# VectorE in written order in the first layer of a two-layer convolution kernel, with earlier loads, a moved gate mix and borders in the background

## The chip, the cores and the metric

The kernel runs on one core of a Trainium2 chip. Its time is the device time of one execution in microseconds. The kernel before took 14336.46 us (median of 3 runs, 14333.49 to 14348.35).

## What is computed

The input x is a batch of 32 images of 8 channels and 256 x 256 pixels in fp32. Layer 0 normalises x in four groups of two channels each (GroupNorm) and makes three things of the result: the outcome of 15 steps of a coupled logistic lattice (each step multiplies g by 1 - g, mixes in a 3 x 3 convolution of each channel with itself and 0.15 of the start image), a small network (3 x 3 convolution to 128 hidden channels, relu, 1 x 1 to 8 channels, sigmoid), and a gate g that chooses between the two.

```python
for _ in range(STEPS):                       # 15
    mapped = R * grid * (1.0 - grid)
    local = _conv(mapped, K_local, groups=C_OUT)
    physics = (1.0 - EPS) * mapped + EPS * local
    grid = (1.0 - BETA) * physics + BETA * drive
cml_out = jnp.clip(grid, 0.0001, 1.0 - 0.0001)
nca_out = jax.nn.sigmoid(_conv(jax.nn.relu(_conv(x, Wp, bp)), Wu, bu))
gin = jnp.concatenate([x, cml_out, nca_out], axis=1)
g = jax.nn.sigmoid(_conv(jax.nn.relu(_conv(gin, Wg1, bg1)), Wg2, bg2))
return g * cml_out + (1.0 - g) * nca_out
```

The result is added to x. Layer 1 normalises again, quantises to integers of at most 127, convolves 3 x 3 to 8 channels and adds once more.

## The kernel before, in words

Layer 0 is one stage and layer 1 the next; each has its own pools of on-chip memory. Images that pass from step to step lie in DRAM scratch tensors: `xp_s` (normalised, split in a high and a low part), `xq_s` (normalised, for the lattice), `cm_s` (lattice result), `nc_s` (network result), `y_s` (layer 0's result). Their border rows are zeroed at the start from a zero tile `zt` by 272 DMAs on ACT's queue (lines 199 and 202). `zt` lies in the preparation pool. The pools of layer 0 are opened later on the same memory, and with the plain pool setting every one of their tiles waits for all users of the preparation pool.

The 32 images are handled in 8 groups of 4. For each group four pieces of work are written as generators:

- `lattice(g)`: for each of 8 channels ("units") 15 steps; a step has three tiles, and for each tile TensorE makes six matmuls (L487) into two PSUM buffers `pt`, VectorE adds the start image (`gt`, L495) and makes the next map (`m_a` or `m_b`, L500), GpSimd clears two columns (L504). After the second and third tile, two DMAs each (`exchange`, L450 and L451) copy neighbouring rows of `m_a` for the next step. `background(3)` issues up to three waiting loads or stores of the lattice after every tile. The next unit's images are loaded from step 7 on.
- `nca(b)`: the network, by pairs of `hidden` matmuls (L567, PSUM buffers `ph` from the same pool of six), relu on ACT (L577), the small second product (L584) and a sigmoid.
- `gate(b)`: ten pairs of strips `p`. `stage` loads the network result `nb`, the lattice result `cq` and the image `xb`, GpSimd rearranges `cq` into `cmb` (L681), VectorE scales `xb` into `xnb` (L700). TensorE makes 18 matmuls from `xnb`, `cmb` and `nb` (L759); relu follows (L771). `finish` of the pair before makes the gate `pg` (L725), sigmoid (L727), on GpSimd `d` = lattice - network (L730) and `f` = x + network (L732), and on VectorE the mix gate * d + f (L734, L735) with its statistics (L743 to L745).
- `normalise(jobs)`: a job is one half (two channel pairs) of one image: load `xr`, statistics (L305), average over partitions with two small matmuls (L313, L324), a power on GpSimd (L327), scaling (L331), a rearranged copy `xq` on ACT (L336), the cast `hi` (L342), the remainder `lo` on GpSimd (L343), and six store DMAs. `hi`, `lo` and `xq` have one buffer each, `xr` four.

`together` mixes the lattice of group g with a filler: the network of group g, the gate of group g - 1 and the normalising of group g + 1. A generator's `yield w` ends a piece that counts w; pieces are drawn so that both sides advance in proportion to planned totals (`T_NCA` 520, `T_GATE` 340, `T_PREP` 34, `T_LATTICE` about 709). Before the first lattice, `prep(0, (0,))` normalises the first half of the channels of four images; their second half comes first in group 0's filler. After the last lattice the last four gates run alone.

TensorE's instructions keep the order in which the program writes them:

```python
one.enter_context(tc.manual_schedule(engines={mybir.EngineType.PE}))
```

All other engines, SP's DMA queue included, are ordered by the framework's scheduler, which may move an instruction ahead of others when it expects its inputs to be ready.

## Time and profile before

| what | value |
|---|---|
| median of 3 runs | 14336.46 us |
| profiled execution | 14416.5 us, span 14414.7 us |
| mean granted TensorE clock | 0.963 |
| TensorE busy | 13267.4 us (92%) |
| VectorE busy | 8213.1 us (57%) |
| ACT busy | 4039.8 us (28%) |
| GpSimd busy | 2445.9 us (17%) |
| L487 lattice matmuls | 5827.0 us from m_a, 5796.6 us from m_b |
| L567 hidden matmuls | 2800.2 and 2675.2 us |
| DMA share of the span, mean | 41.9% on SP's queue, 1.7% on ACT's |

The profile shows one execution. Times in it are microseconds from the span's start. A row of a timeline gives the start, the duration, the engine (SPq is SP's queue as it issues DMAs), the line, the operation, what it writes and reads, how many were merged, and in brackets how long the engine had been idle and what ended that. A row of waits gives who waited for whom, the sum, the number of times and the longest. A row of a window gives each engine's busy time and number of records, then the mean granted TensorE clock and the share and rate of the DMA engines. TensorE's records count each fp32 matmul twice. Lines are those of the kernel before.

### The profile page before, as it was taken

The page shows a single profiled execution, that of the slowest core. Times are in us where ns is not written, and L with a number is a line of the kernel's source. Part 1 is how long each engine was busy: PE and PEld are TensorE (multiplying, and loading weights), DVE is VectorE, ACT ScalarE, POOL GpSimd, SP SyncE. Part 2 cuts the span into 40 slices and gives each one's busy share as a digit, 9 for nine tenths or more (in the row PEclk, how much of TensorE's full clock was granted, in tenths as well). Part 3 has the DMA queues.
Part 4 walks back from the last instruction along what each step waited for, and adds up shares of the span by engine and source line. Part 5 has one row for each costly group of instructions (what it writes and reads, how often), then busy time and mean ns, then how long its engine had stood idle before and what let it go on. Part 6 is the DMA issues. An engine that isn't in the chain of part 4 may idle for free.

```text
span 14414.7 us, 229163 instructions
## 1 busy us (share of the span) xinstructions
PE 13267.4 (92%) x81728; PEld 6423.3 (45%) x81728; DVE 8213.1 (57%) x16290; ACT 4039.8 (28%) x6274; POOL 2445.9 (17%) x4266
## 2 busy tenths in 40 slices
PE   2999999999999999999999999999999999999833
PEld 1554444444444444444444444444444444444311
DVE  3555555555555555555555555555555555555576
ACT  1333232232222222222322223222323222222122
POOL 1111111111111111111111111111111111112300
PEclk9999999999999999999999999999999999999966
DMA  5444444444444444444444434444444433333465
GB/s 148 93 97 92 90 103 106 103 94 100 110 94 100 99 106 94 103 100 95 100 103 107 98 93 106 110 94 94 104 104 98 103 88 88 80 83 78 122 195 176
DMA packets 2259559, 1496.74 MB, mean 104 GB/s; under 512 B 1061248, under 2 KB 2229504, under 8 KB 2258304
## 3 DMA queue, kind: packets, MB, share of 16 engines
q1 hardware_dynamic: 2176976, 1401.95, 41.9%
q10 hardware_dynamic: 81456, 80.12, 1.7%
q8 instruction: 664, 10.88, 0.3%
q14 instruction: 463, 3.79, 0.1%
HBM read 866.48 MB, written 478.69 MB: 93 GB/s over the span
## 4 chain that ended last, share of the span: by engine, by line
PE 70%; DMA 9%; DVE 9%; SPq 5%; issue 3%; POOL 2%; ACT 1%; ACTq 1%; POOLq 0%; DVEq 0%
PE pt L487 31%; PE ph L567 18%; PE pa L759 13%; PE acc L584 7%; DVE gt L495 2%; DMA im<-xp_s 1%; PE pg L725 1%; DMA xp_s<-lo 1%; SPq L545 1%; DVE m_b L500 1%; DMA xb<-in_x_dram 1%; DMA m_a<-m_a 1%; DMA out_dram<-ob 1%; SPq L960 1%; PE pt L953 1%
## 5 line engine op out<-in xcount | busy, mean ns | idle before, releaser
L487 PE MATMUL pt<-m_a,lw 128*64 128x390 f32 x17280 | 5827.0, 497 | 186.4 <-DMA m_a<-m_a 122.4
L487 PE MATMUL pt<-m_b,lw 128*64 128x384 f32 x17280 | 5796.6, 492 | 19.2 <-DVE m_b L410 18.0
L577 ACT ACTIVATE h<-ph,bp_sb 128x512 f32<-128x512 f32 x4096 | 2584.6, 684 | 6491.5 <-PE ph L567 6423.0
L487 PEld LDWEIGHTS pt<-m_a,lw 128*64 128x64 f32 x17280 | 2298.4, 138 | 1884.0 <-issue 1681.2
L487 PEld LDWEIGHTS pt<-m_b,lw 128*64 128x64 f32 x17280 | 2306.6, 138 | 1560.0 <-issue 1423.6
L567 PE MATMUL ph<-im,wp_hi 48*128 48x512 f32 x12288 | 2800.2, 419 | 174.2 <-DVE gt L495 113.1
L567 PE MATMUL ph<-im,wp_lo 48*128 48x512 f32 x12288 | 2675.2, 402 | 0.0
L495 DVE SCALAR_TENSOR_TENSOR gt<-pt,d_b 128x390 f32<-128x390 f32 x2880 | 1605.3, 557 | 1714.7 <-PE pt L487 1711.2
L495 DVE SCALAR_TENSOR_TENSOR gt<-pt,d_a 128x384 f32<-128x384 f32 x2880 | 1580.3, 549 | 1694.5 <-PE pt L487 1694.1
L504 POOL TENSOR_TENSOR m_b<-m_b,junk 128x12 f32<-128x12 f32 x2688 | 795.5, 296 | 8193.8 <-DVE m_b L500 7517.2
L567 PEld LDWEIGHTS ph<-im,wp_hi 48*128 48x128 f32 x12288 | 1417.5, 189 | 1081.7 <-DVE gt L495 303.9
L500 DVE SCALAR_TENSOR_TENSOR m_b<-gt 128x390 f32<-128x390 f32 x2688 | 1546.1, 575 | 44.5 <-DVE gt L495 2.3
L500 DVE SCALAR_TENSOR_TENSOR m_a<-gt 128x384 f32<-128x384 f32 x2688 | 1522.3, 566 | 17.2
L567 PEld LDWEIGHTS ph<-im,wp_lo 48*128 48x128 f32 x12288 | 1417.0, 189 | 217.3
L584 PE MATMUL acc<-h,wu_z 128*32 128x512 f32 x8320 | 1165.6, 603 | 6.1 <-ACT nca L602 5.5
L759 PE MATMUL pa<-xnb,gw 128*64 128x512 f32 (+1 forms) x3840 | 879.9, 588 | 43.7 <-DVE xnb L700 43.5
L759 PE MATMUL pa<-cmb,gw 128*64 128x512 f32 (+1 forms) x3840 | 857.6, 577 | 17.4 <-POOL cmb L681 17.4
L759 PE MATMUL pa<-nb,gw 128*64 128x512 f32 (+1 forms) x3840 | 863.6, 576 | 0.0
L730 POOL TENSOR_TENSOR d<-cmb,nb 128x512 f32<-128x512 f32 x320 | 502.9, 1572 | 1460.6 <-DVE gate L734 1028.5
L700 DVE TENSOR_SCALAR xnb<-xb,sc 128x256 f32<-128x256 f32 x608 | 290.7, 493 | 796.7 <-DMA xb<-in_x_dram 759.5
L953 PE MATMUL pt<-qt,qw 128*128 128x512 bf16 (+1 forms) x960 | 269.5, 451 | 477.0 <-ACT ob L954 425.4
L734 DVE TENSOR_TENSOR gate<-gate,d 128x512 f32<-128x512 f32 x320 | 217.4, 679 | 764.7 <-ACT gate L727 756.7
(132 smaller groups left out, 6928.0 us busy)
## 6 DMA issues: line engine op xcount, KB each, us to landing
im<-xp_s SPq DMA_DIRECT2D x1152, 193.5 KB
im<-xp_s SPq DMA_DIRECT2D x1216, 96.8 KB
d_a<-xq_s SPq DMA_DIRECT2D x2048, 36.0 KB
nb<-nc_s SPq DMA_DIRECT2D x288, 256.0 KB
cq<-cm_s SPq DMA_DIRECT2D x288, 256.0 KB
yb<-y_s ACTq DMA_DIRECT2D x29, 2432.0 KB
xb<-in_x_dram SPq DMA_DIRECT2D x544, 128.0 KB
xp_s<-hi SPq DMA_DIRECT2D x256, 258.0 KB
```

The costliest lines, as they stand in the source:

```text
L487: T.matmul(pt[half], lw[:, c, k, half], beside if part == 2 else own, start=part < 2, stop=part > 0,)
L495: V.scalar_tensor_tensor(gt, pt, FLOOR, d[:, ts, :], ALU.max, ALU.add)
L500: V.scalar_tensor_tensor(to, gt, 1.0, gt, ALU.subtract, ALU.mult)
L504: G.tensor_tensor(edge, edge, junk.unsqueeze(1).to_broadcast([P, 6, 2]), ALU.mult)
L567: T.matmul(ph[:, :n].rearrange("p (h w) -> p h w", w=W), w[64 * i : 64 * i + 48, dx, :], rhs[:, :, dx : dx + W], start=(dx == 0 and w is w ...
L577: S.activation(h[:, :n], ph[:, :n], AF.Relu, bias=bp_sb)
L584: T.matmul(acc[32 * g : 32 * g + 32, :cols], wu_z[:, 24 - 8 * i : 56 - 8 * i], h, start=first, stop=last,)
L700: V.tensor_scalar(xnb[:, k, 1 : 1 + W], xb[:, k, :], sc[:, i : i + 1], sc[:, 1:2], ALU.subtract, ALU.mult,)
L730: G.tensor_tensor(three(d), cmb[:, :n, 1 : 1 + W], nin, ALU.subtract)
L734: V.tensor_tensor(y[:, :cols], gt[:, :cols], d[:, :cols], ALU.mult)
L759: T.matmul(three[half], gw[:, s * 3 + dx, half], t[:, :n, dx : dx + W], start=(i == 0), stop=(i == 8),)
L953: T.matmul(pt, qw[:, dx, :], q[:, k0 : k0 + n, dx : dx + W], start=(dx == 0), stop=(dx == 2))
```

## The change

- The layer-0 stage is in written order for VectorE as well as for TensorE.
- Its pools have `reuse_waits="tile"`: a tile waits only for earlier users of its own bytes. `hp` is opened first. `zt` moves into the constant pool and is 64 wide. `wk1` has 2 buffers.
- Borders are described as short runs (64 elements, or 43 in `xp_s`) of a broadcast `zt`. 16 are issued at the start on ACT; the rest is issued on SP by `background` in group 0, once a second unit has been loaded, when fewer than three lattice DMAs wait.
- A job of `normalise` names its channel pairs; before the first lattice only the first pair of four images is normalised, and the rest of group 0 comes first in its filler. The load (`begin`) is half a piece ahead of the statistics (`take`); the stores are half a piece behind the cast.
- In `gate`, `arrange` takes the work on loaded strips out of `stage` and comes two pieces after the loads; it makes `d` and `f` as well (`f` in place of `xb`). The mix of a pair (`finish`) is written ahead of the next pair's first matmuls, where it was behind the last ones.

```diff
-        one.enter_context(tc.manual_schedule(engines={mybir.EngineType.PE}))
-        pool = lambda name, bufs, **kw: one.enter_context(tc.tile_pool(name=name, bufs=bufs, **kw))
-        xp, sp2, gp, bp2, st = pool("xp", 4), pool("sp2", 1), pool("gp", 3), pool("bp2", 2), pool("st", 2)
-        imp, hp, wk, wk1, np_ = pool("imp", 3), pool("hp", 12), pool("wk", 2), pool("wk1", 1), pool("np", 1)
+        one.enter_context(tc.manual_schedule(engines={mybir.EngineType.PE, mybir.EngineType.DVE}))
+        pool = lambda name, bufs, **kw: one.enter_context(
+            tc.tile_pool(name=name, bufs=bufs, reuse_waits="tile", **kw)
+        )
+        hp, xp, sp2, gp, bp2 = pool("hp", 12), pool("xp", 4), pool("sp2", 1), pool("gp", 3), pool("bp2", 2)
+        st, imp, wk, wk1, np_ = pool("st", 2), pool("imp", 3), pool("wk", 2), pool("wk1", 2), pool("np", 1)
...
+            k = 64 if w == W else 43
+            for row, m in ((0, 1), (257, 5), (262, 5), (267, 1)):
+                borders.append(
+                    (
+                        dram_ap(t, row * n * w, [[w, m * n], [k, w // k], [1, k]]),
+                        zt[: m * n, :k].unsqueeze(1).to_broadcast([m * n, w // k, k]),
+                    )
+                )
+        for _ in range(4 * GB):
+            nc.scalar.dma_start(*borders.pop(0))
...
             def background(n):
                 for _ in range(min(n, len(later))):
                     nc.sync.dma_start(*later.pop(0))
+                    n -= 1
                     issued[0] += 1
+                if g == 0 and units.keys() - {0}:
+                    for _ in range(min(n, len(borders))):
+                        nc.sync.dma_start(*borders.pop(0))
...
                     V.tensor_copy(inner(hi), xr)
                     G.tensor_tensor(inner(lo), xr, inner(hi).bitcast(F32), ALU.subtract)
-                    for h in range(2):
...
-                    yield 1.0
-                ready.add((b, half))
+                    yield 0.5
+                    stores(b, g, xq)
+                    yield 0.5
...
             for job in [*jobs, None]:
                 now = begin(*job) if job else None
-                yield 1.0
+                yield 0.5
                 if ahead:
                     e = scale(*ahead)
                     yield 1.0
                     yield from end(*ahead[:3], e)
-                ahead = now
+                ahead = take(*now) if job else None
+                yield 0.5
...
+        def arrange(xnb, xb, cmb, nb, cq, k0, n, sc):
+            for k in range(n):
+                G.tensor_copy(
+                    cmb[:, k, 1 : 1 + W].rearrange("p (j q) -> p j q", q=4),
+                    cq[:, k, :].rearrange("p (q j) -> p j q", q=4),
+                )
             for k in range(n):
                 i = 2 if k0 + k == 0 else 3 if k0 + k == NB - 1 else 0
                 V.tensor_scalar(
                     xnb[:, k, 1 : 1 + W], xb[:, k, :], sc[:, i : i + 1], sc[:, 1:2],
                     ALU.subtract, ALU.mult,
                 )
-            return xnb, xb, cmb, nb
+            d = wk1.tile([P, 2, W], F32, name="d", tag="d")
+            nin = nb[:, :n, 1 : 1 + W]
+            G.tensor_tensor(d[:, :n, :], cmb[:, :n, 1 : 1 + W], nin, ALU.subtract)
+            G.tensor_tensor(xb[:, :n, :], xb[:, :n, :], nin, ALU.add)
+            return xnb, cmb, nb, d, xb
...
             for p in range(10):
                 n = 2 if p < 9 else 1
-                xnb, xb, cmb, nb = ahead
+                xnb, cmb, nb, d, f = ahead
+                if last:
+                    if done:
+                        nc.sync.dma_start(*done)
+                    done = finish(*last)
...
                 for s, t in ((0, xnb), (1, cmb), (2, nb)):
+                    if s == 2 and p < 9:
+                        ahead = arrange(*ahead)
+                    elif s == 2 and b + 1 in staged:
+                        staged[b + 1] = staged[b + 1][0], arrange(*staged[b + 1][1])
...
-                if last:
-                    if done:
-                        nc.sync.dma_start(*done)
-                    done = finish(*last)
-                if sums:
-                    sums.pop(0)()
-                yield 3.5
-                last = (p, r1, xb, cmb, nb)
+                    if s == 1 and sums:
+                        sums.pop(0)()
+                    if s == 2:
+                        r1 = wk.tile([P, 512], F32, name="r1", tag="r1")
+                        S.activation(r1[:, : n * W], pa[:, : n * W], AF.Relu, bias=bv[:, 0:1])
+                        last = (p, r1, d, f)
+                    yield 3.5 if s == 0 and p else 2.6
...
-        for _ in prep(0, (0,)):
+        for _ in prep(0, ((0,),)):
...
             if g == 0:
-                fill, t = chain(prep(0, (1,)), fill), t + 20.0
+                fill, t = chain(prep(0, ((1,), (2, 3))), fill), t + 30.0
             together(lattice(g), T_LATTICE, fill, t)
+            while borders:
+                nc.sync.dma_start(*borders.pop(0))
```

## The prediction

> **What bounds the kernel now.** I read the page's slices first, then a table of busy time and clock by stage (cut at the first VectorE instruction of each group's lattice), then who TensorE waits for in the six like stages, then VectorE's and TensorE's own timelines at single stalls.
>
> ```profile
> PE   2999999999999999999999999999999999999833
> ...
> PEclk9999999999999999999999999999999999999966
> ```
>
> TensorE is the bound: busy 9 tenths or more from slice 2 to 37, with a thin first slice and a thin end (layer one's follower, which the change leaves alone). So only three things can be won: the start, TensorE's idle time in between, and its clock.
>
> ```profile
> core 0: us, PE busy (x) PEld busy (x) DVE busy (x) ACT busy (x) POOL busy (x), PEclk, DMA share, GB/s
> 0.00:201.00 201.00, 4.51 (x16) 3.93 (x16) 47.89 (x147) 17.60 (x9) 22.88 (x54) 1.00 0.48 141
> 201.00:1679.00 1478.00, 1323.88 (x8468) 693.50 (x8470) 814.07 (x1688) 443.19 (x679) 163.46 (x372) 0.94 0.46 102
> ...
> 3318.00:4987.00 1669.00, 1628.79 (x10104) 791.78 (x10103) 957.09 (x2003) 477.49 (x744) 305.62 (x528) 0.98 0.44 100
> ...
> 11642.00:13250.00 1608.00, 1598.56 (x10081) 764.80 (x10079) 897.07 (x1885) 442.25 (x722) 265.69 (x504) 1.00 0.36 80
> 13250.00:13650.00 400.00, 352.36 (x1704) 127.84 (x1701) 202.48 (x429) 55.51 (x85) 163.77 (x172) 0.94 0.38 109
> ```
>
> Groups 1 to 6 take 1639, 1669, 1665, 1672, 1663 and 1655 us; group 7 takes 1608 with practically the same TensorE records (10,081 against 10,104). It alone has no next group to normalise. What normalising costs the other six through TensorE's idle time and clock is thus 9963 - 6 x 1608 = 315 us; that is the most this stage can give. Who holds TensorE there:
>
> ```profile
> PE ph L567 <- DVE gt L495: 85.4, 121, 3.3
> PE pt L487 <- DMA m_a<-m_a: 75.2, 52, 4.1
> PE pa L759 <- DVE xnb L700: 30.2, 5, 7.1
> PE ph L567 <- ACT gate L727: 16.9, 6, 3.5
> ```
>
> A hidden matmul waits for a PSUM buffer that VectorE has not read yet. Why VectorE is late, at one such stall:
>
> ```profile
> 4086.23 0.56 DVE L495 SCALAR_TENSOR_TENSOR gt<-pt,d_b 128x390 f32<-128x390 f32 x1
> 4091.01 0.69 DVE L342 CAST hi<-xr 128x1024 fp32r<-128x1024 f32 x1 [4.22 <-DMA xp_s<-hi]
> 4091.62 0.56 DVE L500 SCALAR_TENSOR_TENSOR m_b<-gt 128x390 f32<-128x390 f32 x1
> ```
>
> The scheduler put a cast of the normalised image in the middle of a lattice step, and the cast waits for the previous store of its only buffer. VectorE stands still for 4.22 us with ready lattice work behind it.
>
> **The change, part by part.**
>
> *Start.* The first image load waits for every user of the preparation pool, the 272 border DMAs on ACT's queue among them:
>
> ```profile
> 113.88 2.06 SPq L300 DMA_DIRECT2D xr<-in_x_dram  x4
> 117.94 1.29 DVE L305 BATCH_NORM_STATS2 stats<-xr 128x6 f32<-128x512 f32 x2 [85.56 <-DMA xr<-in_x_dram]
> ```
>
> In the changed kernel's instruction list these loads stand right behind the ten weight loads and wait for one earlier DMA only, so they issue near 16 us. The statistics stand behind the gate weights on VectorE, whose timeline reaches them at 27. So the normalising chain starts 118 - 27 = 91 us sooner. Its pace doesn't change: the eight casts of hi before the lattice run from 127.1 to 189.1, 8.9 us each, eight more from 237.1 to 303.6, 9.5 each, set by the one hi buffer and its stores. All 16 still have to pass before the first hidden matmul (316.1); now 4 stand ahead of the lattice and 12 beside it. Last cast: 34 (27, and 7 for one channel pair's chain; two took 9.2) + 3 x 8.9 + 31 (last cast to lattice, 189.1 to 220.3, d_a loads included) + 16 (lattice to the next cast) + 11 x 9.5 = 212 instead of 303.6: 92 us. Beside those casts the list has 6 lattice steps instead of 4, at 5.9 us each: 12 us more. **-104 us**, between -85 and -125.
>
> *Borders.* 19 go out on SP in the start, where SP waits anyway; 237 are put behind the lattice's background DMAs in group 0, up to three a tile. On ACT one such issue took 0.31 to 0.44 us, so 75 to 105 us of SP, whose issues fill 62% of group 0. What is queued behind them is the exchange of m_a, which TensorE waits for when little fill lies between two steps. From the matmul order, 47 of group 0's 120 steps have under 4 us of fill. 237 borders load 26 steps; four in ten of those are short: 10 steps x 1.2 us, and half of these with a clock loss of 3.4 us (below): **+29 us**, from 0 to +80. The new borders go in pieces of 172 and 256 B instead of about 1 KB: some 28,000 more packets. The trace's 256 B packets took 22 ns on average, so over 16 engines that is 38 us of shared transfer time, hidden under a DMA share of 0.46; uncovered it would be those 38.
>
> *VectorE in program order, lattice.* Emission order is gt, m, gt, m, where m needs the gt just before it; the scheduler mostly made gt, gt, m, m. The trace has both. Where m follows its own gt, as at
>
> ```profile
> 284.38 0.56 DVE L500 SCALAR_TENSOR_TENSOR m_a<-gt 128x384 f32<-128x384 f32 x1
> 284.85 0.56 DVE L495 SCALAR_TENSOR_TENSOR gt<-pt,d_b 128x390 f32<-128x390 f32 x1
> 285.44 0.57 DVE L500 SCALAR_TENSOR_TENSOR m_b<-gt 128x390 f32<-128x390 f32 x1
> ```
>
> gt to m is 0.59 us; where they don't depend it is 0.47. The Trainium skill (VectorE: DVE Perf Modes, section "The DRAIN you can't avoid") says the opposite: the pipe empties after each operation whatever the order, and a semaphore between two adds nothing. By that rule this part is free; by the row each tile takes 2.13 us instead of 1.89, against 1.96 of TensorE for its six matmuls. I go with the row: VectorE falls behind by about half a microsecond over a step. What hides it is the fill. An exchange is ready about 3.8 us after a step's last matmul instead of 3.3 (tile two's end at 0.5, two issues of 0.6, some 2 us to land; 1.3 to 3.2 at the stalls that ended at 3378.6 and 4724.3); summing the shortfall of fill against both bounds gives 73 - 50 = 23 us more in group 0, 43 - 29 = 14 in groups 1 to 6, 3 in group 7, and some 15 for clock: **+55 us**. Without any fill it would be 0.5 us x 960 steps.
>
> *VectorE in program order, the rest.* Casts, statistics and image scaling now come at the emitted place, between steps. A unit of prep work is 1/34 of a group, about 48 us; stores are emitted half a unit after their cast and the next cast another half, so a store has some 24 us where 8.9 were enough. In exchange the lattice now queues behind VectorE's wait for GpSimd's power (1.0 us at most so far; 4.1 if GpSimd has just begun a pair's copies, d and f). At 56 such jobs and GpSimd 18% busy, 56 x 0.18 x 2 is 20 us of VectorE time under 7 us fills: zero, uncovered 20. Of the 85.4 + 16.9 us of stalls (the ACT ones come from xq, whose single buffer waits alike) and what they cost in clock, I take away three quarters. The clock:
>
> ```profile
> 2287.05 0.77 PE L567 MATMUL ph<-im,wp_hi 48*128 48x512 f32 x1 [1.77 <-DVE gt L495]
> ```
>
> After this stall of 1.77 us the clock records read 0.5 for 6.8 us. The Trainium skill (TensorE: Matmul & The Clock Gate, section "Part 1: The HAM clock gate") wants a whole idle window of about 3.4 us before the clock halves; by that, hardly a stall here would cost more than its own length, and this part would be worth 77 us. In this trace 56 half-clock spells, 300 us together, fall in the six groups, nearly all behind stalls of 1.2 to 3.3 us; the measurement decides. At half speed that is 150 us lost; the spells nearest to stalls on gt and gate hold 80 + 17. So 0.75 x (102 + 97) = **-149 us**. The first gate image of a group (xnb, 39 us and 17 of clock) now has a piece between load and use: half, **-28**. In group 0 the same casts cost 20 us of stalls and about 10 of clock: **-20**.
>
> *The gate's mix.* It moves behind the next pair's first matmuls, d and f behind none: with two d buffers GpSimd makes them a piece ahead. Mix costs 0.68 + 0.94 + 0.69 + 0.64 + 0.65 = 3.6 us of VectorE, unchanged. It waits for sigmoid, and lattice work is queued behind it. After pg TensorE has six matmuls (2.5 us) and a tile (2.0) before VectorE is wanted; sigmoid 1.2 and mix 3.9 exceed this by 0.6 us at most. In the matmul order only 20 of 271 mixes are followed by a fill too short for that: 14 us, mostly in the sum above already. **0**; without that cover 3.6 us each, and some gain if earlier d and f ever mattered (-10).
>
> Tail (13250 to 13650): the 17 us wait for the last lattice output stays; **0**, within 15 either way.
>
> Sum: -104 + 29 + 55 - 149 - 28 - 20 = -217 us. The profiled execution took 14416.5 us with a span of 14414.7; less 217 is 14,200. The runs' median, 14336.46, lies 0.55% lower, so I subtract the same amount there: **14,120 us**.
>
> **Rivals.** (1) *Late exchange takes the place of the casts.* When gt is in time, m_a is next: 75 us of stalls are its own already, behind SP's queue, and stores, image loads and borders remain on SP. If it eats what the middle groups win, the start remains: 14,336 - 104 + 29 = 14,261. For it: exchange stalls follow bursts of SP issues. Against: group 7 has the same fill and none of these waits. (2) *All groups run like the last.* -104 - 315 + 60 gives 13,977 (the 60: borders and lattice order, less group 0's casts). Against: stores and xq still go through SP and ACT. (3) *Slower: ACT holds the mix.* ACT stays with the scheduler; xq (2.1 us) and four relus (0.65 each) can precede a sigmoid, and in program order the lattice behind the mix waits too. From about 3 us of delay the exchange misses the 7.1 us fill; each such mix then costs 1.3 us plus 3.4 of clock. A quarter of 271 mixes is +320; with start and half the casts' gain left, 14,336 + 320 - 104 - 75 = 14,477. Against: ACT is 29% busy in these groups. (4) *The loads don't move:* then -217 + 104, 14,223; the list speaks against it.
>
> **Numbers.** Forecast 0.5, rival 1 0.25, rival 2 0.13, rival 3 0.08, rival 4 0.04. The range reaches from just below rival 2 to the top of rival 1's spread: 13,950 to 14,310. A difference under 0.2% can't be told from no change here: faster 0.88, same 0.04, slower 0.08.
>
> **What would show it.** First statistics at 27 us, lattice near 92, first hidden matmul near 225. Dependent gt and m throughout. In groups 1 to 6 hi waits gone from VectorE, ph waits under 30 us, clock 0.99, about 1630 us each. Wrong: m_a waits well above 75 us, group 0 longer by more than the start saves, or mixes waiting on ACT with TensorE idle behind.

## The result, and the profile after

The kernel after takes 14144.33 us (median of 4 runs, 14141.83 to 14145.41), against 14337.08 us for the kernel before on the same chip (14333.49 to 14348.35): a ratio of 0.9864, 95% interval 0.9847 to 0.9881. The forecast was 14,120. The profiled execution of after lies on its median (span 14140.0 us). The profiled execution of before that the prediction read was 80 us longer than its kernel's median; a second one (14339.24 us, span 14337.4) lies on the median, and all stages below are compared with that second one.

| stage (us, profiled) | before | after |
|---|---|---|
| start to the first lattice instruction on VectorE | 198 | 81 |
| group 0 | 1471 | 1555 |
| groups 1 to 6 | 9909 | 9724 |
| group 7 | 1601 | 1596 |
| last lattice matmul to layer one | 406 | 431 |
| layer one | 752 | 753 |

The start wins 117, the six like groups win 185, group 0 loses 84 and the end loses 25. The page's slices after show the shorter start, and the clock at 9 tenths or more from slice 2 to 38:

```profile
PE   5899999999999999999999999999999999999733
PEclk8999999999999999999999999999999999999966
```

The same kind of table by stage as before, first of after, then of the second execution of before:

```profile
core 0: us, PE busy (x) PEld busy (x) DVE busy (x) ACT busy (x) POOL busy (x), PEclk, DMA share, GB/s
0.00:81.25 81.25, 4.66 (x16) 4.01 (x16) 33.59 (x127) 9.41 (x5) 13.47 (x50) 1.00 0.80 167
81.25:1636.00 1554.75, 1356.06 (x8485) 713.08 (x8487) 869.66 (x1701) 452.26 (x683) 146.05 (x380) 0.93 0.47 107
...
4870.00:6490.00 1620.00, 1595.05 (x10100) 771.70 (x10098) 1014.10 (x2001) 476.78 (x744) 279.70 (x528) 1.00 0.45 103
11360.00:12956.00 1596.00, 1583.04 (x10079) 756.75 (x10076) 950.34 (x1888) 442.63 (x722) 239.25 (x504) 1.00 0.36 81
```

```profile
198.40:1669.00 1470.60, 1323.99 (x8465) 691.06 (x8467) 813.87 (x1686) 443.11 (x679) 163.32 (x372) 0.94 0.45 103
...
4959.00:6612.00 1653.00, 1614.93 (x10100) 783.22 (x10098) 959.02 (x2002) 477.44 (x744) 307.48 (x528) 0.99 0.43 101
```

The like group shown falls from 1653 to 1620 us with the same TensorE records (10,100). VectorE is busier for practically the same number of instructions (2,001 and 2,002), 1014 us against 959: the first sign that its order costs something. In group 0 TensorE's idle time (length less busy time) rises from 147 to 199 us.

Who holds TensorE in groups 1 to 6 after (who for whom, sum, times, longest):

```profile
PE pt L511 <- DMA m_a<-m_a: 59.3, 55, 4.0
PE pa L799 <- DVE xnb L729: 30.3, 12, 5.0
PE pg L758 <- ACT r L812: 17.0, 22, 0.9
PE ph L591 <- ACT h L601: 16.3, 6, 2.7
PE ph L591 <- DVE gt L519: 11.0, 18, 0.9
```

The hidden matmuls' wait for `gt`, the largest row of before, is down to 11.0. In the second execution of before it was:

```profile
PE ph L567 <- DVE gt L495: 76.6, 116, 3.4
```

VectorE's own timeline after, at one cast:

```profile
5388.08 0.81 DVE L365 TENSOR_SCALAR xr<-xr,mean_x,rstd_x 128x1024 f32<-128x1024 f32 x1 [0.82 <-POOL rstd_x L362]
5388.92 0.69 DVE L376 CAST hi<-xr 128x1024 fp32r<-128x1024 f32 x1
5389.53 2.60 DVE L729 TENSOR_SCALAR xnb<-xb,sc 128x256 f32<-128x256 f32 x2
```

The cast of `hi` waits for nothing now. All this looks as the prediction said. The experiments show that it came about in another way.

### The profile page after: what moved, and what is told of

Its sections match the earlier page's. It is cut to its first block, busy times and chain, and to the rows that moved or that the text cites. A ratio compares the mean times of both kernels' runs of the same rounds, so it can differ in the third digit from the quotient of the medians.

```text
span 14140.0 us, 227821 instructions
## 1 busy us (share of the span) xinstructions
PE 13141.8 (93%) x81744; PEld 6342.4 (45%) x81744; DVE 8640.5 (61%) x16310; ACT 4037.6 (29%) x6274; POOL 2233.9 (16%) x4270
## 4 chain that ended last, share of the span: by engine, by line
PE 80%; DMA 6%; DVE 6%; SPq 4%; issue 2%; ACT 1%; POOL 0%; POOLq 0%; DVEq 0%; ACTq 0%
PE pt L511 35%; PE ph L591 19%; PE pa L799 15%; PE acc L608 7%; DVE gt L519 2%; PE pg L758 2%; DMA im<-xp_s 2%; DVE m_a L524 1%; DMA out_dram<-ob 1%; SPq L998 1%; DMA m_a<-m_a 1%; PE pt L991 1%; SPq L464 1%; DMA yb<-y_s 1%; SPq L569 1%
## 5 line engine op out<-in xcount | busy, mean ns | idle before, releaser
L511 PE MATMUL pt<-m_b,lw 128*64 128x384 f32 x17280 | 5785.2, 491 | 20.5 <-DVE m_b L430 18.4
L591 PE MATMUL ph<-im,wp_hi 48*128 48x512 f32 x12288 | 2628.3, 412 | 77.8 <-DMA im<-xp_s 44.6
L591 PE MATMUL ph<-im,wp_lo 48*128 48x512 f32 x12288 | 2522.2, 396 | 0.0
L528 POOL TENSOR_TENSOR m_b<-m_b,junk 128x12 f32<-128x12 f32 x2688 | 607.5, 226 | 8831.5 <-DVE m_b L524 8304.6
L524 DVE SCALAR_TENSOR_TENSOR m_b<-gt 128x390 f32<-128x390 f32 x2688 | 1571.5, 585 | 232.1 <-DVE gt L519 4.6
L591 PEld LDWEIGHTS ph<-im,wp_hi 48*128 48x128 f32 x12288 | 1250.9, 186 | 917.1 <-DVE gt L519 231.6
L524 DVE SCALAR_TENSOR_TENSOR m_a<-gt 128x384 f32<-128x384 f32 x2688 | 1583.5, 589 | 92.6
L591 PEld LDWEIGHTS ph<-im,wp_lo 48*128 48x128 f32 x12288 | 1250.9, 187 | 229.4
L812 ACT ACTIVATE r<-pa,bv 128x512 f32<-128x512 f32 x320 | 213.2, 666 | 1708.6 <-PE pa L799 1708.1
```

The lines of the kernel that those rows point to most:

```text
L511: T.matmul(pt[half], lw[:, c, k, half], beside if part == 2 else own, start=part < 2, stop=part > 0,)
L524: V.scalar_tensor_tensor(to, gt, 1.0, gt, ALU.subtract, ALU.mult)
L528: G.tensor_tensor(edge, edge, junk.unsqueeze(1).to_broadcast([P, 6, 2]), ALU.mult)
L591: T.matmul(ph[:, :n].rearrange("p (h w) -> p h w", w=W), w[64 * i : 64 * i + 48, dx, :], rhs[:, :, dx : dx + W], start=(dx == 0 and w is w ...
L812: S.activation(r1[:, : n * W], pa[:, : n * W], AF.Relu, bias=bv[:, 0:1])
```

## The experiments

My theory going in was that the written order of VectorE, with the casts out of the lattice step, makes the gain of the like groups, and the background borders the loss of group 0. The table gives each kernel's stages in its profiled execution, and its median.

| kernel | start | group 0 | 1 to 6 | group 7 | end | median |
|---|---|---|---|---|---|---|
| before, second execution | 198 | 1471 | 9909 | 1601 | 406 | 14339 |
| after | 81 | 1555 | 9724 | 1596 | 431 | 14144 |
| after, VectorE free | 81 | 1539 | 9657 | 1587 | 430 | 14063 |
| after, both sums first | 82 | 1537 | 9645 | 1588 | 433 | 14036 |
| after, borders on ACT at the start | 270 | 1490 | 9717 | 1594 | 431 | 14262 |
| after, first half | 116 | 1523 | 9719 | 1595 | 432 | 14141 |
| before, VectorE written | 204 | 1480 | 10452 | 1681 | 399 | 14969 |
| before, new normalise | 194 | 1452 | 9934 | 1607 | 405 | 14362 |
| before, new gate | 198 | 1463 | 9707 | 1593 | 428 | 14140 |
| before, new gate, mix at the end | 199 | 1465 | 9756 | 1584 | 406 | 14148 |
| before, mix moved only | 199 | 1465 | 9767 | 1589 | 423 | 14201 |
| before, scaling later only | 198 | 1471 | 9801 | 1588 | 409 | 14221 |
| after with three edits | 77 | 1481 | 9658 | 1589 | 406 | 13967 |

**Before, once more.** No edit.

> The kernel before, profiled a second time. The first profiled execution lay 80 us over the median of its runs (14416.5 against 14337), while the profiled execution of after lies on its median. If that was one unlucky execution, the second lies between 14,330 and 14,360, and the stages show where the 80 us were: I expect a length of about 1,650 us in groups 1 to 6 in place of 1,659, and the start and the end as they were. If it repeats 14,416, the profiler itself costs the scheduled VectorE order more than it costs the written one.

14339.24 us. The 80 us were one execution's: groups 1 to 6 took 9909 us in place of 9963, and 43 spells at half clock (229 us) in place of 56 (300 us).

**After, VectorE left to the scheduler.**

```diff
-        one.enter_context(tc.manual_schedule(engines={mybir.EngineType.PE, mybir.EngineType.DVE}))
+        one.enter_context(tc.manual_schedule(engines={mybir.EngineType.PE}))
```

> The kernel after, with VectorE's order left to the scheduler again (PE alone in written order); the loads ahead, the mix in the next pair, the tile waits, the first pair and the borders stay. My theory, that the written order itself is what keeps casts and normalising work out of a lattice step, says groups 1 to 6 go back from about 1,621 us each to 1,650 or more and the time to about 14,300. The rival, that the loads a piece ahead and the moved mix bring the gain whatever the order, says 14,144 to 14,180.

14062.71 us (14046.23 to 14072.84), 0.9805 of before (0.9792 to 0.9819), 82 us faster than after. Neither case had this: the written order does not bring the gain, it costs 82 us. The scheduler lets the casts wait for their stores as before:

```profile
DVE xnb L729 <- DMA xb<-in_x_dram: 425.1, 138, 11.8
DVE gate L762 <- ACT gate L760: 277.0, 90, 5.6
DVE hi L376 <- DMA xp_s<-hi: 103.3, 34, 6.3
```

These are VectorE's waits in groups 1 to 6. The 103 us of cast waits are nearly the 133 us of before, and the groups are still 252 us shorter. So those waits were not what TensorE paid for. My theory fell here.

**After, both sums ahead of both products.** Written order stays; a tile runs gt, gt, m, m.

```diff
+                        gts = []
                         for s, a2b, n, pt in jobs:
...
                             V.scalar_tensor_tensor(gt, pt, FLOOR, d[:, ts, :], ALU.max, ALU.add)
+                            gts.append(gt)
+                        for (s, a2b, n, pt), gt in zip(jobs, gts):
...
                             V.scalar_tensor_tensor(to, gt, 1.0, gt, ALU.subtract, ALU.mult)
```

> The kernel after, with the two sums of a lattice tile ahead of its two products on VectorE (gt, gt, m, m in place of gt, m, gt, m), so that no instruction directly follows the one whose result it reads. By the 0.59 against 0.47 us of the prediction the tile gets 0.24 us shorter; the theory that this length is on the path in part says PE's waits for m_a in groups 1 to 6 fall from 59 us to about 30, and group 0 gains 15 to 25 us: 14,080. The rival, that the exchange and not VectorE releases the tiles, says 14,130 to 14,160.

14035.75 us (14027.52 to 14040.21), ratio 0.9787 (0.9774 to 0.98): 108 us below after, more than expected. After's own timeline shows why:

```profile
5378.02 0.56 DVE L519 SCALAR_TENSOR_TENSOR gt<-pt,d_a 128x384 f32<-128x384 f32 x1 [4.05 <-PE pt L511]
5378.62 0.56 DVE L524 SCALAR_TENSOR_TENSOR m_a<-gt 128x384 f32<-128x384 f32 x1
5379.09 0.56 DVE L519 SCALAR_TENSOR_TENSOR gt<-pt,d_b 128x390 f32<-128x390 f32 x1
5379.75 0.57 DVE L524 SCALAR_TENSOR_TENSOR m_b<-gt 128x390 f32<-128x390 f32 x1
5380.24 0.55 DVE L519 SCALAR_TENSOR_TENSOR gt<-pt,d_a 128x384 f32<-128x384 f32 x1
```

From a gt to its own m it is 0.60 and 0.66 us, from an m to the next gt 0.47 and 0.49: a tile takes 2.22 us. In this experiment the steps within a tile are 0.48 us (gt to gt), 0.47 (gt to m) and 0.50 (m to m) on average, some 1.9 for a tile, and TensorE needs 1.96 for a tile; VectorE's busy time in a like group is back at 958 us. TensorE's waits in groups 1 to 6 of the experiment:

```profile
PE pt L511 <- DMA m_a<-m_a: 45.8, 45, 3.0
PE pa L803 <- DVE xnb L733: 24.9, 6, 4.5
```

The wait for the exchange falls from 59.3 to 45.8, less than expected; with the other rows TensorE's idle time falls by 41 us, and the half-clock loss by 10, of the 79 us that groups 1 to 6 win. The rest lies within TensorE's busy records. The same turn also reads the tile's second PSUM buffer sooner: the second gt starts 0.48 us behind the first in place of 1.07. No run divides this from the shorter tile. Either way gt, m, gt, m costs 108 us, and the written order as such gains 27 over the scheduler's.

**After, all borders on ACT's queue at the start.**

```diff
-        for _ in range(4 * GB):
+        while borders:
             nc.scalar.dma_start(*borders.pop(0))
```

> The kernel after, with all 272 border writes on ScalarE's queue at the start, as the kernel before issues them, and none on SyncE. My theory, that the 256 writes on SyncE's queue hold exchanges and image loads in group 0, says group 0 falls from 1,554 us to about 1,490, the start rises by no more than 10, and the time is about 14,090. The rival, that group 0 lost its 76 us to the second to fourth channel pairs moved into it and to the written order, says group 0 stays above 1,535 and the time stays within 20 us of 14,144.

14262.12 us (14255.59 to 14265.76), ratio 0.9946 (0.9932 to 0.9959). Half right: group 0 falls by 65 us to 1490. But the lattice starts at 270 in place of 81. ACT's queue in this experiment (start, length, engine, line, what):

```profile
147.33 99.52 ACTq L211 DMA_DIRECT2D y_s<-zt  x128
246.88 1.28 ACT L370 ACT_TABLE_LOAD   x1 [246.88 <-DMA y_s<-zt]
248.17 2.01 ACT L370 ACTIVATE xq<-xr 128x1024 f32<-128x1024 f32 x1
```

ACT makes `xq`, from which the lattice is loaded, and here it does so behind all the border issues. With short runs on ACT's queue the lattice starts later than in before (198), free loads or not: short runs had to leave ACT too. (Long runs left on ACT beside the freed loads were not run.) In group 0 TensorE's wait for the exchange is 40.0 us here and 68.6 in after, so part of the 65 us is the exchange behind the borders. And one issue takes 99.52 / 128 = 0.78 us here. In after, on SyncE, likewise, where the long runs of before had taken 0.31 to 0.35:

```profile
702.40 6.16 SPq L469 DMA_DIRECT2D cm_s<-zt  x8
```

```profile
59.84 0.31 ACTq L199 DMA_DIRECT2D nc_s<-zt  x1
60.19 1.04 ACTq L202 DMA_DIRECT2D nc_s<-zt  x3
```

**After, the whole first half ahead of the first lattice.**

```diff
-        for _ in prep(0, ((0,),)):
+        for _ in prep(0, ((0, 1),)):
...
-                fill, t = chain(prep(0, ((1,), (2, 3))), fill), t + 30.0
+                fill, t = chain(prep(0, ((2, 3),)), fill), t + 30.0
```

> The kernel after with both pairs of the first half normalised ahead of the first lattice, as before, in place of one pair. Eight casts of hi instead of four stand ahead of the lattice, 8.9 us each: the lattice starts near 81 + 36 = 117. If those casts cost less beside the lattice than ahead of it, group 0 gets only some 15 to 20 us shorter and the time is about 14,165. If they cost the same on either side, the time stays at 14,144; if group 0 suffers from them more than the start, it is 14,120 or less.

14140.83 us (14135.78 to 14144.87), 3 us from after. The start is 35 us longer, as worked out, and group 0 is 32 us shorter. A cast costs the same on either side: taking only one pair first is worth nothing.

**Before, VectorE in written order and nothing else.**

```diff
-        one.enter_context(tc.manual_schedule(engines={mybir.EngineType.PE}))
+        one.enter_context(tc.manual_schedule(engines={mybir.EngineType.PE, mybir.EngineType.DVE}))
```

> The kernel before with VectorE in written order and nothing else changed. As emitted there, statistics, scaling of xb and mix stand directly behind the load or the sigmoid that they wait for, with lattice work behind them: 271 xb loads of about 2 us, 271 mixes behind relu, product and sigmoid. The theory that the order alone is worth nothing, or less, says 14,450 or more, with waits for VectorE's xnb and gate in TensorE's list. The prediction's theory, that the written order keeps the casts out of the lattice step, says 14,150 to 14,250.

14968.93 us (14954.85 to 14973.98), ratio 1.0433 (1.0418 to 1.0447). TensorE's first row in groups 1 to 6, then VectorE's waits for loads:

```profile
PE ph L567 <- DVE gt L495: 421.7, 372, 12.5
```

```profile
DVE xnb L700 <- DMA xb<-in_x_dram: 1019.6, 170, 17.3
```

In written order an instruction that waits for a load holds the lattice behind it. In after VectorE's wait for `xb` is 1.9 us. So the loads ahead and the later scaling take away the largest wait that the written order has by itself: they are a condition of it, and it is not the source of the gain.

**Before, the new normalise alone.** Load, statistics and stores are emitted as in after; a job is still half an image.

```diff
...
                     G.tensor_tensor(inner(lo), xr, inner(hi).bitcast(F32), ALU.subtract)
+                    yield 0.5
+                    stores(b, g, xq)
+                    yield 0.5
...
-                ahead = now
+                ahead = take(*now) if job else None
+                yield 0.5
...
```

> The kernel before with the new normalise alone: a job is still half an image, VectorE stays with the scheduler, but the load is half a piece ahead of the statistics and the stores half a piece behind the cast. The written order turned out to be worth little (after with VectorE free: 14,063; written with both sums first: 14,036), so the 183 us that groups 1 to 6 won must come from what was emitted elsewhere. If it is the normalising pieces, the waits of hidden matmuls for gt in groups 1 to 6 fall from 76 us to under 25, these groups from 1,651 us to about 1,628, and the time to about 14,200. If it is the gate, the time stays within 30 us of before (14,337).

14361.63 us (14336.52 to 14383.46), ratio 1.0015 (1.0009 to 1.0022). No gain, a small loss: the hidden matmuls' wait for gt is 89.5 us in place of 76.6.

**Before, the new gate alone.** `stage`, `arrange`, `gate` and two buffers of `d` as in after, all else as before.

> The kernel before with the new gate alone: arrange a piece behind the loads, the mix ahead of the next pair's first matmuls, two buffers of d, VectorE still with the scheduler. If the gate is the smaller part, the 40 us of waits for xnb and the 14 for the sigmoid go and the time is about 14,270; if it is the larger part, the waits for gt fall as well (the mix no longer stands between lattice tiles) and the time is 14,200 or less. If neither this nor the new normalise moves much alone, the two hold each other's gain.

14140.39 us (14117.49 to 14146.59), ratio 0.9856 (0.9842 to 0.9869). This part alone, which the prediction put at 28 us for the first image and at nothing for the mix, makes a difference of 200 us: groups 1 to 6 win 202, groups 0 and 7 win 8 each, and the end loses 22. VectorE's casts still wait 75 us for their stores here. What was in TensorE's way can be seen on VectorE in before, at a stall of 2.71 us that ended at 9323.92:

```profile
9317.35 0.15 DVE L810 TENSOR_SCALAR rstd_y<-pm 128x1 f32<-128x1 f32 x1
9318.17 0.16 DVE L826 TENSOR_TENSOR dev_y<-dv,rstd_y 128x1 f32<-128x1 f32 x1 [0.67 <-POOL rstd_y L811]
9318.61 0.69 DVE L734 TENSOR_TENSOR gate<-gate,d 128x512 f32<-128x512 f32 x1 [0.27 <-ACT gate L727]
9319.33 0.69 DVE L735 TENSOR_TENSOR gate<-gate,f 128x512 f32<-128x512 f32 x1
9319.94 0.56 DVE L495 SCALAR_TENSOR_TENSOR gt<-pt,d_b 128x390 f32<-128x390 f32 x1
9320.41 0.68 DVE L743 BATCH_NORM_STATS2 st_a<-gate 128x6 f32<-128x512 f32 x1
9321.01 0.67 DVE L744 TENSOR_REDUCE mx<-gate 128x1 f32<-128x512 f32 x1
9321.60 0.68 DVE L745 TENSOR_REDUCE mn<-gate 128x1 f32<-128x512 f32 x1
9322.19 1.20 DVE L500 SCALAR_TENSOR_TENSOR m_b<-gt 128x390 f32<-128x390 f32 x1
9323.32 0.55 DVE L495 SCALAR_TENSOR_TENSOR gt<-pt,d_a 128x384 f32<-128x384 f32 x1
```

The mix, with the sums of layer one ahead of it, stands in the middle of a lattice tile: 1.3 us of mix ahead of a gt, the three statistics, 1.8 us, between this gt and its m, then the m (1.20 us in place of 0.56, beside a GpSimd instruction that makes `f`), and the next gt is late. There is hardly an idle gap in it, so a search for waits doesn't find it. It is no single case. Of the 237 mixes in groups 1 to 6 of before, 119 have statistics between a gt and its m; with the new gate none of 238 has. And of the 119 stalls of TensorE on a gt or m there (81 us), 87 (51 us) have a mix in the 8 us ahead, 53 of these (42 us) with less than half a microsecond of idle time before it; only 6 (13 us) have a cast.

I shared each stall on a gt or m of groups 1 to 6 in before out over the other work that VectorE did in the 8 us ahead of it, with half of the half-clock time that followed: mix 69 us, normalising 42, scaling 17, sums 11; stalls directly on xnb come to 61, directly on the sigmoid to 28. This is an estimate: weighed a little differently, it gives mix 77 and normalising 33.

One thing it leaves open. Group 7 has the same gate, with statistics between a gt and its m in 23 of 40 cases, and yet TensorE idles only 8.5 us there and the new gate wins only 8. So the old place costs much only where the next group is normalised beside it: VectorE is busy 58 us longer there (957 against 899). How the two come together no run shows.

**Before, the mix moved and nothing else; and the new gate with the mix back at the end.** Two kernels, each the other's complement within the new gate.

```diff
                 xnb, xb, cmb, nb = ahead
+                if last:
+                    if done:
+                        nc.sync.dma_start(*done)
+                    done = finish(*last)
...
-                if last:
-                    if done:
-                        nc.sync.dma_start(*done)
-                    done = finish(*last)
...
```

> The kernel before with one thing moved: the mix of a pair (finish) stands ahead of the next pair's first matmuls in place of behind its last ones; loads, scaling of xb, d and f stay where they were, VectorE stays with the scheduler. The new gate as a whole gave 200 us. My theory now is that the place of the mix does it: behind the pair's last matmuls its sigmoid queues behind their relu on ACT, VectorE waits with the lattice behind it, and TensorE's stalls on gt, which I had put down to the casts, come from there. It says VectorE's waits for the sigmoid fall from 614 us to about 310 in groups 1 to 6, TensorE's waits for gt from 76 to about 25, and the time to 14,140 to 14,180. The rival, that scaling and loads of the next pair (arrange) do it, says 14,300 or more.

> The complement: the new gate on the kernel before, but with the mix back behind the pair's last matmuls; arrange two pieces behind the loads and the early d and f stay. If the place of the mix is the cause, the waits for gt stay above 60 us and the time is 14,290 to 14,340, with only the first gate image's 29 us of waits gone. If arrange is the cause, the time is 14,140 to 14,180.

The mix alone: 14200.84 us (14188.25 to 14211.73), ratio 0.9902 (0.9885 to 0.9918), 142 us. The rest alone: 14148.17 us (14145.23 to 14158.64), ratio 0.9867 (0.9852 to 0.9881), 194 us. Each gives most of the whole, so both expectations were wrong in their either-or. TensorE's waits in groups 1 to 6, first with the mix moved, then with everything but the mix:

```profile
PE pa L763 <- DVE xnb L700: 32.3, 5, 6.6
PE pg L725 <- ACT r L775: 27.6, 41, 0.9
PE pt L487 <- DMA m_a<-m_a: 25.3, 31, 3.1
...
PE ph L567 <- DVE gt L495: 19.9, 34, 2.5
```

```profile
PE ph L567 <- DVE gt L495: 46.3, 56, 2.5
PE pt L487 <- DMA m_a<-m_a: 41.2, 35, 3.6
```

Moving the mix takes the wait for gt from 76.6 to 19.9 and leaves xnb. Moving the rest takes xnb away altogether and leaves more than half of the wait for gt. Their gains overlap: together they give 200, not 336. The statistics stand between a gt and its m in 5 of 238 mixes with the first and in 102 with the second. In the sharing above, the mix goes from 69 us to 7 and to 48.

**Before, the scaling later, with the rearranging of `cq` on GpSimd, and nothing else.**

```diff
...
                 for s, t in ((0, xnb), (1, cmb), (2, nb)):
+                    if s == 2 and p < 9:
+                        ahead = arrange(*ahead)
...
```

> The kernel before with the scaling of xb and the rearranging of cq (xnb, cmb) two pieces behind their loads, and nothing else of the new gate: d, f, the mix and the sums of layer one stay behind the pair's last matmuls, VectorE stays with the scheduler. The new gate without the moved mix gave 194 us. Of TensorE's idle time and half-clock time in groups 1 to 6 of before, 61 us have xnb as their direct releaser, 17 a gt behind a VectorE that waits for xb, 31 a gt behind the sums. If each part only takes away its own rows, this kernel gains the first two, 60 to 80 us, and comes to about 14,270, and the rest of the 194 lies with the sums and with d and f. If the later scaling alone empties the place where VectorE's waiting work piles up, it gains 140 us or more: 14,200 or less. If nothing comes of it (14,320 or more), it was the sums, or d and f.

14220.77 us (14212.65 to 14249.48), ratio 0.9918 (0.9905 to 0.9932): 122 us, between the two cases. TensorE's idle and half-clock time in groups 1 to 6 falls by 73 us, near the 60 to 80 of the first case; another 35 us of these groups lie within TensorE's busy records, and group 7 gains 13. The wait for gt hardly falls:

```profile
PE ph L567 <- DVE gt L495: 71.6, 81, 3.0
```

So the scaling was late for the gate's own matmuls: their direct waits for xnb (28.9 us in before) are gone. The 73 us between this kernel and the new gate without the moved mix belong to the early `d` and `f`, to the moved sums or to the last store of an image, which is issued a piece later; no run divides these.

**After with three edits.** Both sums first, as above; the borders at most one a tile, each group only those that the next one needs; the mix behind the next pair's first two matmuls.

```diff
...
-                if g == 0 and units.keys() - {0}:
-                    for _ in range(min(n, len(borders))):
+                if g or units.keys() - {0}:
+                    for _ in range(min(n, 1, max(0, len(borders) - keep[g]))):
                         nc.sync.dma_start(*borders.pop(0))
...
+                        if i == 0 and last:
+                            if done:
+                                nc.sync.dma_start(*done)
+                            done = finish(*last)
                         i += 1
...
```

> After with three edits: the two sums ahead of the two products (14,036 by itself); the borders on SyncE one per tile at most, each group writing only those that the next group needs (48, 48, 32 and then 32 a group); the mix behind the first two matmuls of the next pair in place of ahead of them. By the theory that the border issues cost group 0 its 64 us, group 0 falls from 1,537 to about 1,485, and the later groups gain at most 3 us each. By the theory that the product of the gate waits for relu because it follows it directly, the end from the last lattice matmul to layer one falls from 433 to about 410 us, and groups 1 to 6 lose their 18 us of waits for relu. Together about 13,960. If the mix, 0.9 us later, makes VectorE late for the lattice, groups 1 to 6 get longer by some 5 us each, and the time is about 14,000.

13967.30 us (13962.52 to 13975.14), ratio 0.974 (0.9725 to 0.9754): faster than both kernels, 177 us below after. Against the kernel with both sums first, group 0 falls by 56 us and the end by 27; groups 1 to 6 get 2 us longer each, by the mix or by the borders that are now among them. In the end stage the gate's product had waited for relu. The row here, and then in after:

```profile
PE pg L766 <- ACT r L820: 5.5, 11, 0.6
```

```profile
PE pg L758 <- ACT r L812: 34.5, 42, 0.9
```

## Why the time came out as forecast, though a main step was wrong

The forecast sum was -217 us; the medians differ by 193. The steps, one by one:

- **Start, -104: right in size, and only half of its cause.** The loads did move: the first statistics stand at 31.4 us (27 forecast, 118.4 in before), the lattice starts at 81 (92), the first hidden matmul at 226 (225). (The 316.1 that the step starts from is the second hidden matmul of before; the first stood at 305.3.) The step counted the pool's waits and the four casts; it left out that `xq` stands behind the borders on ACT: with short runs left there the lattice starts at 270. The four casts in place of eight were worth nothing.
- **Borders, +29: mis-sized, 65 us.** The mechanism was right: with the borders off SyncE group 0 gets 65 us shorter. The term that failed is the price of an issue: 75 to 105 us for 237 of them, from issues of long runs at 0.31 to 0.44 us. In short runs one took 0.75 us on average (0.60 in `xp_s`), and the 256 on SyncE 186 us together: about twice the price, and about twice the step.
- **Written order in the lattice, +55: right cause, mis-sized, 108 us.** The step took 0.59 us from gt to m and 2.13 for a tile; the chip took 0.59 and 0.64 on average in groups 1 to 6 of after (0.60 and 0.66, 2.22 for the tile, where it is shown). The term that failed is the sum of shortfalls against the exchange, 23 + 14 + 3 us: group 0 gave back 17 and group 7 gave 8, but groups 1 to 6 gave back 79, and only 13.5 of these as waits for the exchange. The Trainium skill (VectorE: DVE Perf Modes, section "The DRAIN you can't avoid") says that the next operation doesn't start until the pipe is empty and that a semaphore between two costs nothing extra, which read by itself makes this free. The same section adds that an operation that is not held starts earlier, but prices no pair in which the second reads the first's result. Here independent ones start 0.47 us apart, before the first has ended (0.56), and turning m and gt round, with the same instructions, gave 108 us.
- **Casts out of the lattice step, -149: the step that failed.** It said that the stalls on gt come from casts waiting for their store. The scheduler's order keeps these waits (103 us) and the groups are shorter all the same, the new normalise alone costs 21 us, and the written order alone 629. I had one stall with a cast in it, and took three quarters of the row for its kind; in the execution that I read, 6 of 122 stalls on a gt or m have a cast in the 8 us ahead, 15 of 86 us, and 89 have a mix, 53 us. By the sharing above, normalising makes about 40 of the 330 us of idle and half-clock time in these groups. The gain of this size came from the gate.
- **First gate image, -28: mis-sized, in a part worth much more.** Later scaling, with `cq`, gives 122 us: it holds for every pair, and the step counted only the first image of a group.
- **Gate's mix, 0: wrong.** Moved alone it gives 142 us; on top of the later scaling, the early d and f and the moved sums it is worth only 8 more, which the two intervals don't tell from nothing. The step asked what the new place costs and never what the old one did: in the scheduler's order its last three instructions stood between a gt and its m in half of the cases. A gain had been bounded at 10 us.
- **Casts of group 0, -20:** the new normalise alone shortens group 0 by 19 us, which fits; the wait for gt there falls from 18.4 to 6.5 us.
- **End, 0 within 15: missed by 10.** It lost 25 us. The gate's product `pg` now directly follows the relu that it needs, 0.8 us in each of 42 waits, and moving the mix back by two matmuls gave 27 us.

The medians of the runs add up in this way, taken in this order: 14,340 for before, less 200 for the gate is 14,140; start, borders, tile waits and normalise together take off 77 more (after with VectorE free, 14,063); the written order with both sums first another 27 (14,036); gt, m, gt, m puts 108 on: 14,144. So the gate's 200 us stood in for the 149, 28 and 20 that I had given mostly to the casts; a lattice order and borders that cost twice what I had taken made up for what else was won. That these errors cancelled was luck: without the gate, the summed steps would have been far off.

Of the rivals, the late exchange (14,261) did not come: the wait for m_a is 59.3 us, 56.5 in the second execution of before. All groups like the last (13,977) came near in the groups, at 1621 us against 1596. ACT did not hold the mix: VectorE's waits for the sigmoid fell from 642 to 318 us. The loads moved.

The prediction put the 315 us that groups 1 to 6 take over group 7 (303 in the second execution) down to normalising. That reading was too simple: the new gate alone won back 202 of them, with the normalising as it was.

What stays open: how the 73 us divide between d, f, sums and the last store; what shortens TensorE's busy records, its half-clock time aside, by some 30 to 90 us in these groups; why the gate's old place costs so little in group 7; and which part makes groups 1 to 6 of after with VectorE free 50 us shorter than those of the new gate alone.

## What to carry to other kernels

A stall's releaser names the instruction that was late, and not the work that made it late: read the engine's whole list ahead of several stalls, its busy instructions as well as its gaps, before a cause gets the row. When a step of a kernel is moved, price the old place as carefully as the new one. And run each part alone: here one part gave 200 us by itself, as much as the whole change, another cost 629, and two of them overlapped by 136.

## What the hardware showed beyond this

The issue of a border DMA got longer when its rows were cut into pieces of a broadcast source, and hardly with the number of its runs. Whole rows of 1 KB took 0.31 us for 8 rows and 0.30 to 0.35 for 40; rows in four pieces of 256 B took 0.69 us for 8 rows (32 runs) and 0.78 to 0.80 for 40 (160 runs), on ACT's queue as on SyncE's. So 32 short runs cost twice what 40 long ones did; whether the pieces or the broadcast did it, no run divides.

Of the 56 half-clock spells in groups 1 to 6 of the execution that the prediction read, 42 follow a stall of 1.2 to 3.3 us as the longest in the 7 us ahead, 3 a shorter one and 11 a longer one, up to 7.1. So half clock does follow short stalls here, but "nearly all" was three quarters.

VectorE's product m, which reads the same SBUF tile twice, got longer beside a GpSimd instruction. In after, groups 1 to 6, m_a (L524) took 0.56 us by itself and 0.93 on average in the 191 cases that overlapped one, m_b 0.57 and 0.99 in 93 cases; gt, with one input in PSUM, took 0.55 to 0.56 in both. One such case, VectorE's row and then GpSimd's:

```profile
5392.64 1.18 DVE L524 SCALAR_TENSOR_TENSOR m_b<-gt 128x390 f32<-128x390 f32 x1
```

```profile
5392.22 1.18 POOL L736 TENSOR_TENSOR xb<-xb,nb 128x512 f32<-128x512 f32 x1 [0.23 <-DVE xnb L729]
```

The Trainium skill (SBUF — State Buffer, section "Who interferes with whom") says that a VectorE instruction with two SBUF inputs contends with a GpSimd instruction that reads SBUF, and that one with at most one SBUF input, outside the 2-port modes, doesn't; these rows agree. A short GpSimd instruction costs little: with both sums first 1,086 m_a overlap one, mostly the 0.2 us that clear two columns (L528 in after), and take 0.59 us on average. 284 cases of some 0.4 us are about 110 us of VectorE; what of it reaches TensorE no run shows.
